# Moving the closing residual addition of a 30-step recurrence into its middle, and splitting the last stores over two queues

## The chip, the cores and the metric

The kernel runs on one core of a Trainium2 chip. The metric is the device time of one execution in microseconds (us), as the median of several runs. The engines are named as the profile names them: PE (TensorE matrix products; PEld its weight loads), DVE (VectorE), ACT (ScalarE), POOL (GpSimd) and SP (SyncE, which here only issues transfers; SPq is its queue).

## The reference

Rows of a 3327 x 256 matrix `x` go through two layers. Each layer is a graph attention over a 3327 x 3327 adjacency matrix, added to `x`, and then a network, also added to `x`. In layer 0 the network is a mixture of 16 experts; in layer 1 it is a recurrence of 30 steps. The change touches only the end of layer 1, which is, cut to what matters:

```python
def step(h, _):
    h = h + 0.01 * jnp.tanh(h)
    h = h * jax.nn.sigmoid(h)
    h = _layernorm(h, ln_w, ln_b)          # eps = 1e-5
    h = jnp.einsum('bsc,dc->bsd', h, W) + b
    return (h, None)
x = x + _L1_gnn_ref(_layernorm(x), adj, ...)
h, _ = jax.lax.scan(step, _layernorm(x), None, length=30)
x = x + h                                  # the closing addition
```

So the output is the last state of the recurrence plus the rows of `x` as they stood before the recurrence began.

## The kernel before

**Layout.** The rows lie in 26 tiles of 128 partitions x 256 features, all float32, resident in the on-chip tile `x`. For the recurrence they are handled in 7 groups: groups 0 to 5 have four tiles, group 6 has two. `COUNT` is 7, `LAST` is 30 x 7 = 210, and a number `at` from 0 to 209 stands for one group in one step. The state in `x` is kept multiplied by S = 100.

**Before the recurrence.** When the attention of layer 1 has finished some row tiles, `begin_state` stores them to the DRAM tensor `kept` (L1012, on SP) and normalizes them in place. `kept` is what the closing addition needs later. The adjacency matrix lies on chip in the tile `adjT` (13 x 3328 bfloat16 numbers on each partition) until the attention of layer 1 is through.

**One group in one step** is a `Group` object with these parts:
- `tanh` (L1050, ACT) writes `th`; `add` (L1053, POOL) adds the state to it, a 128 x 1024 addition of float32; `silu` (L1057, ACT) writes `z`.
- `measure` (L1062, L1065, DVE) takes mean and variance; `invert` (L1070 and L1071, POOL) raises variance plus eps to the power -1/2, in two small instructions, into `rr`.
- The transposed `z` is made in one of two ways. Groups 0, 2, 4 and 6 use `turn_here`: transposes on PE (L1081), copied by ACT (L1083). Groups 1, 3 and 5 use `turn_away`: ACT packs the bytes (L1090), SP stores them to DRAM (L1091) and loads them back with a transposing transfer (L1095) into `zTa`, of which there are two buffers.
- `product` (L1105, PE) multiplies by the 256 x 256 matrix `wc` into the PSUM tile `po`, of which there are two buffers. `evict` (L1115, DVE) scales each tile by `rr`, adds the bias `bb` (already times S) and writes the state back into `x`.

**Order.** The last loop of the program fixes the order of work. At each `at` it emits, in this order: `evict` of at-1, `invert` of at+3, `silu` of at+4, `turn_here` of at+2, `turn_away` and `measure` of at+4, `tanh` of at+6, `add` of at+5, `product` of at. From the second step on, `put` and `tc.keep_in_program_order` hold each engine's instructions to that order, so an instruction that waits holds back everything behind it on its engine. Transfers of `turn_away` are not held to it, but SP also issues its queue in order.

**The last step.** For `at >= LAST - COUNT`, `evict` goes on: SP loads the group's rows of `kept` into a tile `old` (L1122, two buffers), DVE computes state / S + old with one instruction over the whole group (L1123), and `move_pairs` stores the result to `out` on SP (L77). Groups 0 to 5 are one store each; group 6, which holds the ragged end of the 3327 rows, is three: 112 row pairs, 15 row pairs, and a single row.

Of the kernel before, what the change touches and what calls it, by code (L numbers as in the profile page):

```python
# [11 lines left out]
F32 = mybir.dt.float32  # L12
I32 = mybir.dt.int32
I16 = mybir.dt.int16
BF16 = mybir.dt.bfloat16
FP8 = mybir.dt.float8e4
AF = mybir.ActivationFunctionType
ALU = mybir.AluOpType
# [3 lines left out]
P = 128  # L22
ALPHA = 0.2
EPS = 1e-5
N_STEPS = 30
S = 100.0
G = 4
# [4 lines left out]
def gat_moe_gat_recurrent_ffn(ctx: ExitStack, tc: tile.TileContext, a: dict, out: bass.AP):  # L32
    nc = tc.nc
    N, D = a["x"].shape
    KD = D // P
    NT = (N + P - 1) // P
    NP = NT * P
    PAIRS = NT // 2
# [6 lines left out]
    groups = [range(t, min(t + G, NT)) for t in range(0, NT, G)]  # L45
# [25 lines left out]
    if REST < P:  # L71
        nc.vector.memset(x[:, NT - 2, :], 0.0)

    def move_pairs(dram, tile, c0, c1, into_dram):

        def move(dst, src):
            nc.sync.dma_start(*((dst, src) if into_dram else (src, dst)))  # L77

        full = min(c1, PAIRS - 1)
        if full > c0:  # L80
            move(
                dram[c0 * 2 * P : full * 2 * P, :].rearrange("(t p b) d -> p t (b d)", p=P, b=2),
                tile[:, : 2 * (full - c0), :].rearrange("p (t b) d -> p t (b d)", b=2),
            )
        if c1 == PAIRS:
            base, last = (PAIRS - 1) * 2 * P, 2 * (PAIRS - 1 - c0)
            for r0, r1 in spread(REST // 2):
                move(
                    dram[base + 2 * r0 : base + 2 * r1, :].rearrange("(p b) d -> p (b d)", b=2),
                    tile[r0:r1, last : last + 2, :].rearrange("p b d -> p (b d)"),  # L90
                )
            if REST % 2:
                move(dram[base + REST - 1 : base + REST, :], tile[REST // 2 : REST // 2 + 1, last, :])
# [212 lines left out]
    graph = ctx.enter_context(tc.tile_pool(name="graph", bufs=1))  # L306
    adj_pairs = graph.tile([P, PAIRS, NP], BF16, name="adjT")
    adjT = adj_pairs.bitcast(FP8).rearrange("p c (i b) -> p c i b", b=2)
# [714 lines left out]
    with ExitStack() as st:  # L1023
        ps_t = st.enter_context(tc.tile_pool(name="ps3t", bufs=2, space=PSUM))
        turns = cycle((ps, ps_t))
        ps_o = st.enter_context(tc.tile_pool(name="ps3o", bufs=2, space=PSUM))
        last_p = st.enter_context(tc.tile_pool(name="last", bufs=2))

        apart = [dram.tile([G * P, 2, D], I16, name=f"apart{q}") for q in range(2)]
        apart_p = st.enter_context(tc.tile_pool(name="apart", bufs=2))  # L1030

        AWAY = (1, 3, 5)
        COUNT = len(groups)
        LAST = N_STEPS * COUNT

        class Group:

            def __init__(self, at):
                self.at = at
                self.ts = groups[at % COUNT]  # L1040
                self.n = len(self.ts)
                self.hs = x[:, self.ts[0] : self.ts[0] + self.n, :]
                self.away = at % COUNT in AWAY and at > 1

            def put(self, ins):
                return tc.keep_in_program_order(ins) if self.at >= COUNT else ins

            def tanh(self):
                self.th = steps["th"].tile([P, G, D], F32, name="th")[:, : self.n, :]
                self.put(nc.scalar.activation(self.th, self.hs, AF.Tanh, scale=1.0 / S))  # L1050

            def add(self):
                self.put(nc.gpsimd.tensor_tensor(self.th, self.th, self.hs, ALU.add))  # L1053

            def silu(self):
                self.z = steps["z"].tile([P, G, D], F32, name="z")[:, : self.n, :]
                self.put(nc.scalar.activation(self.z, self.th, AF.Silu, scale=1.0 / S))  # L1057

            def measure(self):
                stats = narrow.tile([P, G, 6], F32, name="stats")  # L1060
                for j in range(self.n):
                    self.put(nc.vector.bn_stats(stats[:, j, :], self.z[:, j, :]))  # L1062
                self.v = narrow.tile([P, G, 2], F32, name="v")
                for j in range(self.n):
                    self.put(nc.vector.bn_aggr(self.v[:, j, :], stats[:, j, :]))  # L1065

            def invert(self):
                self.r = narrow.tile([P, G], F32, name="rr")
                r = self.r[:, : self.n]
                self.put(nc.gpsimd.tensor_scalar(r, self.v[:, : self.n, 1], EPS, None, op0=ALU.add))  # L1070
                self.put(nc.gpsimd.tensor_tensor(r, r, neg_half[:, : self.n], ALU.pow))  # L1071

            def turn_here(self):
                pool = next(turns)
                zT = steps["zT"].tile([P, G, KD, P], F32, name="zT")
                for c in range(self.n // 2):
                    pt = pool.tile([P, 2, KD, P], F32, name="bank")
                    for j in range(2):
                        for k in range(KD):
                            (tc.keep_in_program_order if self.at > 1 else lambda ins: ins)(  # L1080
                                nc.tensor.transpose(pt[:, j, k, :], self.z[:, 2 * c + j, k * P : (k + 1) * P], ident)  # L1081
                            )
                    self.put(nc.scalar.copy(zT[:, 2 * c : 2 * c + 2, :, :], pt))  # L1083
                self.zT = lambda j, k: zT[:, j, k, :]

            def turn_away(self):
                n = self.n
                parts = apart_p.tile([P, G, 2, D], I16, name="parts")[:, :n]
                here = apart[self.at % COUNT // 2 % 2][: n * P]
                self.put(nc.scalar.copy(parts, self.z.bitcast(I16).rearrange("p j (d b) -> p j b d", b=2)))  # L1090
                nc.sync.dma_start(  # L1091
                    here.rearrange("(j p) b d -> p j (b d)", p=P), parts.rearrange("p j b d -> p j (b d)")
                )
                zT = apart_p.tile([P, KD, G * P], F32, name="zTa")
                nc.sync.dma_start(  # L1095
                    zT.bitcast(I16)[:, :, : n * 2 * P], here.rearrange("t b d -> (t b) d"), transpose=True
                )
                self.zT = lambda j, k: zT[:, k, j * P : (j + 1) * P]

            def product(self):  # L1100
                self.po = ps_o.tile([P, G, D], F32, name="po")
                for j in range(self.n):
                    for k in range(KD):
                        tc.keep_in_program_order(
                            nc.tensor.matmul(  # L1105
                                self.po[:, j, :], lhsT=self.zT(j, k), rhs=wc[:, k, :],
                                start=(k == 0), stop=(k == KD - 1),
                            )
                        )

            def evict(self):
                ts, n = self.ts, self.n
                for j in range(n):
                    self.put(
                        nc.vector.scalar_tensor_tensor(  # L1115
                            self.hs[:, j, :], self.po[:, j, :], self.r[:, j : j + 1], bb, op0=ALU.mult, op1=ALU.add
                        )
                    )
                if self.at >= LAST - COUNT:
                    here = slice(ts[0] * P, (ts[-1] + 1) * P)  # L1120
                    old = last_p.tile([P, G, D], F32, name="old")
                    nc.sync.dma_start(old[:, :n, :], kept[here, :].rearrange("(t p) d -> p t d", p=P))  # L1122
                    nc.vector.scalar_tensor_tensor(  # L1123
                        self.hs, self.hs, 1.0 / S, old[:, :n, :], op0=ALU.mult, op1=ALU.add
                    )
                    move_pairs(out, self.hs, ts[0] // 2, (ts[-1] + 1) // 2, True)

        live = {}

        def on(at, *what):  # L1130
            if 0 <= at < LAST:
                if at not in live:
                    live[at] = Group(at)
                for w in what:
                    w(live[at])

        for at in range(-6, LAST + 2):
            on(at - 1, Group.evict)
            live.pop(at - 1, None)
            on(at + 3, Group.invert)  # L1140
            on(at + 4, Group.silu)
            on(at + 2, lambda g: g.away or g.turn_here())
            on(at + 4, lambda g: g.away and g.turn_away())
            on(at + 4, Group.measure)
            on(at + 6, Group.tanh)
            on(at + 5, Group.add)
            on(at, Group.product)


# [47 lines left out]
```

## Time and profile before

| What | Value |
|---|---|
| median of 3 runs | 1867.72 us (1865.54 to 1868.72) |
| the profiled execution: its own time / its span | 1862.0 us / 1860.3 us |
| busy shares of the span | PE 97%, PEld 89%, DVE 69%, ACT 64%, POOL 50% |
| recurrence, from its first transposes on PE | 1085 us to the end |
| stretch 1400 to 1600 us: busy us of 200 | PE 200.0, ACT 173.3, DVE 166.8, POOL 185.8 |
| last 29.8 us: busy us | PE 20.4, DVE 20.7, POOL 6.1, ACT 5.1 |
| granted PE clock, mean | 0.996 |

Times in the traces are microseconds from the start of the span, of one execution. In a timeline line the columns are: start, duration of the (possibly merged) entry, engine, line of the kernel, operation, output <- inputs, shapes, and how many instructions were merged; the bracket at the end is the time for which the engine stood idle before it and what ended that idle time.

### The profile page before, as it was taken

How to read it: one execution, taken by the hardware profiler on the slowest of the kernel's cores; microseconds unless marked ns; L12 is line 12 of the kernel's file. 1: busy time of each engine (PE TensorE's matmuls, PEld its weight loads, DVE VectorE, ACT ScalarE, POOL GpSimd, SP SyncE). 2: the span in 40 equal slices, each digit the busy share in tenths (PEclk: the TensorE clock that was granted, in tenths of full speed). 3: DMA queues.
4: the chain of work that ended last, by engine and by line, in shares of the span. 5: the costliest groups of instructions: out<-in, count | busy, mean ns of one | idle time of the engine just before them, and what ended most of it. 6: DMA issues, size and time to landing. Idle time of an engine off the chain costs nothing.

```text
span 1860.3 us, 32198 instructions
## 1 busy us (share of the span) xinstructions
PE 1809.2 (97%) x11212; PEld 1653.9 (89%) x11212; DVE 1284.7 (69%) x3829; ACT 1186.9 (64%) x1498; POOL 939.3 (50%) x864
## 2 busy tenths in 40 slices
PE   7999999999999998899999999999999999999997
PEld 6999999998999998688888888888888888888886
DVE  7888888852222222666776778888888888888887
ACT  2877777641111111556666678888888888888884
POOL 3010212255333331101111159999999999999994
PEclk9999999999999999999999999999999999999999
DMA  8898260169999885400000035554555455555557
GB/s 175 114 122 99 57 100 22 61 224 298 339 338 336 298 284 166 151 14 17 21 15 17 17 108 125 124 127 125 118 132 117 123 133 125 121 121 125 125 127 202
DMA packets 377309, 253.97 MB, mean 137 GB/s; under 512 B 238821, under 2 KB 336924, under 8 KB 377146
## 3 DMA queue, kind: packets, MB, share of 16 engines
q1 hardware_dynamic: 361026, 219.04, 43.1%
q0 software_dynamic: 11440, 28.09, 8.8%
q10 hardware_dynamic: 4680, 4.76, 0.8%
q8 instruction: 91, 1.49, 0.3%
q14 instruction: 72, 0.59, 0.1%
HBM read 168.19 MB, written 76.49 MB: 132 GB/s over the span
## 4 chain that ended last, share of the span: by engine, by line
PE 67%; issue 10%; DVE 6%; POOL 5%; DMA 5%; ACT 0%; SPq 0%; POOLq 0%; DVEq 0%; ACTq 0%
PE po L1105 35%; PE acc L286 24%; PE bank L1081 5%; DVE pT L281 3%; POOL given L855 2%; POOL rb L761 2%; DMA given<-wh,to 2%; DMA wh<-in_w_dram 1%; DMA old<-kept 1%; DMA lists<-pair,ati 1%; PE bank L835 1%; PE acc L163 1%; PE bank L526 1%; POOL rstd L121 1%; PE bank L148 0%
## 5 line engine op out<-in xcount | busy, mean ns | idle before, releaser
L276 ACT ACTIVATE e<-rb,minus,full 128x384 f32<-128x384 f32 (+3 forms) x494 | 400.1, 823 | 166.7 <-DVE pT L281 150.6
L1053 POOL TENSOR_TENSOR th<-th,x 128x1024 f32<-128x1024 f32 (+1 forms) x210 | 465.1, 2215 | 16.0 <-ACT th L1050 14.4
L281 DVE SCALAR_TENSOR_TENSOR pT<-e,part,adjT 128x384 f32<-128x384 f32 (+3 forms) x494 | 383.3, 780 | 118.8 <-PE acc L286 103.4
L1115 DVE SCALAR_TENSOR_TENSOR x<-po,rr,bb 128x256 f32<-128x256 f32 x780 | 323.0, 475 | 104.2 <-PE po L1105 67.3
L1105 PE MATMUL po<-wc,zT 128*128 128x256 f32 x1696 | 385.9, 379 | 1.2 <-DVE x L1115 1.2
L1105 PEld LDWEIGHTS po<-wc,zT 128*128 128x128 f32 x1696 | 315.1, 190 | 40.7 <-issue 1.6
L1105 PE MATMUL po<-wc,zTa 128*128 128x256 f32 x1424 | 321.9, 379 | 0.0
L286 PE MATMUL acc<-wh,pT 128*128 128x129 f32 x2704 | 309.8, 276 | 2.1 <-DVE pT L281 2.1
L286 PEld LDWEIGHTS acc<-wh,pT 128*128 128x128 f32 x2704 | 305.0, 192 | 2.7 <-DVE pT L281 2.5
L1105 PEld LDWEIGHTS po<-wc,zTa 128*128 128x128 f32 x1424 | 268.3, 190 | 35.3
L286 PE MATMUL acc<-s_wh,pT 128*128 128x257 f32 x1352 | 295.2, 381 | 3.5 <-DVE pT L281 3.3
L286 PEld LDWEIGHTS acc<-s_wh,pT 128*128 128x128 f32 x1352 | 256.0, 190 | 42.1 <-DVE pT L281 6.3
L1062 DVE BATCH_NORM_STATS2 stats<-z 128x6 f32<-128x256 f32 x780 | 275.1, 413 | 20.7 <-ACT z L1057 20.6
L1057 ACT ACTIVATE z<-th 128x1024 f32<-128x1024 f32 (+1 forms) x210 | 207.9, 990 | 76.9 <-POOL th L1053 76.7
L121 POOL TENSOR_TENSOR rstd<-ve,neg_half 128x4 f32<-128x4 f32 (+3 forms) x28 | 30.8, 1101 | 409.5 <-DVE ve L119 326.1
L1050 ACT ACTIVATE th<-x 128x1024 f32<-128x1024 f32 (+1 forms) x210 | 209.8, 1000 | 27.0 <-DVE x L1115 24.1
L1071 POOL TENSOR_TENSOR rr<-rr,neg_half 128x4 f32<-128x4 f32 (+1 forms) x210 | 208.4, 992 | 17.5
L1090 ACT COPY parts<-z 128x2048 int16<-128x2048 int16 x89 | 169.1, 1900 | 5.9 <-PE acc L286 4.0
L881 ACT ACTIVATE e<-bank 128x512 f32<-128x512 f32 x61 | 36.4, 597 | 196.3 <-PE bank L835 183.5
L885 DVE TENSOR_TENSOR pT<-e,bank 128x512 f32<-128x512 f32 x61 | 41.9, 688 | 167.5 <-PE bank L835 167.4
L835 PEld LDWEIGHTS bank<-hT,wh 128*128 128x128 f32 x1280 | 149.3, 192 | 4.9 <-ACT hT L827 1.4
L835 PE MATMUL bank<-hT,wh 128*128 128x128 f32 x1280 | 150.5, 275 | 2.4 <-DMA wh<-in_w_dram 2.4
(196 smaller groups left out, 1640.0 us busy)
## 6 DMA issues: line engine op xcount, KB each, us to landing
wh<-in_w_dram SPq DMA_DIRECT2D x120, 512.0 KB
apart<-parts SPq DMA_DIRECT2D x89, 512.0 KB
first_set<-in_w_dram SPq DMA_DIRECT2D x63, 512.0 KB
in_bytes<-in_adj_dram POOLq DMA_DIRECT2D x3, 2496.0 KB, 28.7
x<-in_x_dram SPq DMA_DIRECT2D x6, 512.0 KB
kept<-x SPq DMA_DIRECT2D x8, 384.0 KB
old<-kept SPq DMA_DIRECT2D x6, 512.0 KB
out_dram<-x SPq DMA_DIRECT2D x6, 512.0 KB
```

The lines of the kernel that those rows point to most:

```text
L276: nc.scalar.activation(e[:, : n * P], rb[:, : n * P], AF.Relu, scale=sc.full[:, j, h : h + 1], bias=sc.minus[:, j, h : h + 1],)
L281: masked = nc.vector.scalar_tensor_tensor(pT[:, : n * P], e[:, : n * P], sc.part[:, j, h : h + 1], adjT[:, j // 2, ts[0] * P : (ts[-1] + 1 ...
L286: nc.tensor.matmul(po[c], lhsT=pT[:, c * P : (c + 1) * P], rhs=wh[:, j, h, :], start=(j == 0 and c % per_bank == 0), stop=(j == NT - 1), s ...
L835: nc.tensor.matmul(p[:, f, :], lhsT=w[:, k, f * P : (f + 1) * P], rhs=hT[:, k, :], start=(k == 0), stop=(k == KD - 1),)
L1050: self.put(nc.scalar.activation(self.th, self.hs, AF.Tanh, scale=1.0 / S))
L1053: self.put(nc.gpsimd.tensor_tensor(self.th, self.th, self.hs, ALU.add))
L1057: self.put(nc.scalar.activation(self.z, self.th, AF.Silu, scale=1.0 / S))
L1062: self.put(nc.vector.bn_stats(stats[:, j, :], self.z[:, j, :]))
L1071: self.put(nc.gpsimd.tensor_tensor(r, r, neg_half[:, : self.n], ALU.pow))
L1090: self.put(nc.scalar.copy(parts, self.z.bitcast(I16).rearrange("p j (d b) -> p j b d", b=2)))
L1105: nc.tensor.matmul(self.po[:, j, :], lhsT=self.zT(j, k), rhs=wc[:, k, :], start=(k == 0), stop=(k == KD - 1),)
L1115: nc.vector.scalar_tensor_tensor(self.hs[:, j, :], self.po[:, j, :], self.r[:, j : j + 1], bb, op0=ALU.mult, op1=ALU.add)
```

## The change

Three things are altered.

1. The rows of `kept` are no longer loaded in the last step. A new function `old_rows(at)`, called once per `at` between `add` and `product`, loads one group's rows in each of the steps 6 to 12 (at the place `at % 7 == 2`, on SP), and in each of the steps 8 to 14, at the same place, adds `beside` to one group's rows on POOL. `beside` is the bias divided by S, made once by DVE. The rows lie in the room of `adjT`, which is taken again for this; the pool `last` goes. (`spaces` is defined and not used.)
2. In the last step `invert` multiplies variance plus eps by S x S, so that `rr` comes out divided by S, and `evict` adds the group's prepared rows in the place of the bias. The addition over the whole group (L1123) goes. In all other steps the first instruction of `invert` now multiplies by 1.0, where it had no second operation.
3. The stores of the last step take the queues of SP and ACT in turn, beginning with SP for each group. Only group 6 has more than one store, so its second one (15 row pairs) goes to ACT's queue.

```diff
-    def move_pairs(dram, tile, c0, c1, into_dram):
+    def move_pairs(dram, tile, c0, c1, into_dram, queues=(nc.sync,)):
+        queues = cycle(queues)
         def move(dst, src):
-            nc.sync.dma_start(*((dst, src) if into_dram else (src, dst)))
+            next(queues).dma_start(*((dst, src) if into_dram else (src, dst)))
...
-        last_p = st.enter_context(tc.tile_pool(name="last", bufs=2))
...
+        space = graph.tile([P, PAIRS, NP], BF16, name="adjT").rearrange("p c n -> p (c n)").bitcast(F32)
...
+                self.last = at >= LAST - COUNT
...
             def invert(self):
...
-                self.put(nc.gpsimd.tensor_scalar(r, self.v[:, : self.n, 1], EPS, None, op0=ALU.add))
+                self.put(nc.gpsimd.tensor_scalar(r, self.v[:, : self.n, 1], EPS, S * S if self.last else 1.0, op0=ALU.add, op1=ALU.mult))
...
             def evict(self):
-                ts, n = self.ts, self.n
-                for j in range(n):
+                ts = self.ts
+                for j in range(self.n):
+                    plus = olds[self.at % COUNT][:, j, :] if self.last else bb
                     self.put(
                         nc.vector.scalar_tensor_tensor(
-                            self.hs[:, j, :], self.po[:, j, :], self.r[:, j : j + 1], bb, op0=ALU.mult, op1=ALU.add
+                            self.hs[:, j, :], self.po[:, j, :], self.r[:, j : j + 1], plus, op0=ALU.mult, op1=ALU.add
                         )
                     )
-                if self.at >= LAST - COUNT:
-                    here = slice(ts[0] * P, (ts[-1] + 1) * P)
-                    old = last_p.tile([P, G, D], F32, name="old")
-                    nc.sync.dma_start(old[:, :n, :], kept[here, :].rearrange("(t p) d -> p t d", p=P))
-                    nc.vector.scalar_tensor_tensor(
-                        self.hs, self.hs, 1.0 / S, old[:, :n, :], op0=ALU.mult, op1=ALU.add
-                    )
-                    move_pairs(out, self.hs, ts[0] // 2, (ts[-1] + 1) // 2, True)
+                if self.last:
+                    move_pairs(out, self.hs, ts[0] // 2, (ts[-1] + 1) // 2, True, (nc.sync, nc.scalar))
+
+        beside = rec.tile([P, 1, D], F32, name="prod")
+        nc.vector.tensor_scalar(beside[:, 0, :], bb, 1.0 / S, None, op0=ALU.mult)
+        olds = [
+            space[:, (8 + i) * G * D : (9 + i) * G * D].rearrange("p (j d) -> p j d", d=D)[:, : len(ts), :]
+            for i, ts in enumerate(groups)
+        ]
+
+        def old_rows(at):
+            step, i = divmod(at, COUNT)
+            if i == 2 and 6 <= step < 6 + COUNT:
+                ts = groups[step - 6]
+                here = slice(ts[0] * P, (ts[-1] + 1) * P)
+                tc.keep_in_program_order(
+                    nc.sync.dma_start(olds[step - 6], kept[here, :].rearrange("(t p) d -> p t d", p=P))
+                )
+            if i == 2 and 8 <= step < 8 + COUNT:
+                old = olds[step - 8]
+                tc.keep_in_program_order(
+                    nc.gpsimd.tensor_tensor(old, old, beside.to_broadcast([P, old.shape[1], D]), ALU.add)
+                )
...
             on(at + 5, Group.add)
+            old_rows(at)
             on(at, Group.product)
```

More of the change, by code (lines that the diff above doesn't have):

```diff
@@ L1026, in gat_moe_gat_recurrent_ffn @@
         ps_o = st.enter_context(tc.tile_pool(name="ps3o", bufs=2, space=PSUM))
-        last_p = st.enter_context(tc.tile_pool(name="last", bufs=2))
         apart = [dram.tile([G * P, 2, D], I16, name=f"apart{q}") for q in range(2)]
         apart_p = st.enter_context(tc.tile_pool(name="apart", bufs=2))
+        space = graph.tile([P, PAIRS, NP], BF16, name="adjT").rearrange("p c n -> p (c n)").bitcast(F32)
+        spaces = [space[:, i * G * D : (i + 1) * G * D] for i in range(8)]
         AWAY = (1, 3, 5)
```

## The prediction

> **What bounds the kernel now.** I read the page first, then the timeline of the recurrence's start, one steady step, and the last 20 us.
>
> ```profile
> PE 1809.2 (97%) x11212; PEld 1653.9 (89%) x11212; DVE 1284.7 (69%) x3829; ACT 1186.9 (64%) x1498; POOL 939.3 (50%) x864
> PE   7999999999999998899999999999999999999997
> POOL 3010212255333331101111159999999999999994
> ```
>
> PE is full, so work spared on another engine is worth something only where PE waits: here, at the end. But in the recurrence POOL, 50% over the span, is at 9 tenths as well, and the change gives POOL more to do there. So I looked at how much room POOL has. Its timeline (only POOL's entries) where the recurrence settles:
>
> ```profile
> 1099.95 2.38 POOL L1053 TENSOR_TENSOR th<-th,x 128x1024 f32<-128x1024 f32 x1
> ...
> 1118.33 1.28 POOL L1053 TENSOR_TENSOR th<-th,x 128x512 f32<-128x512 f32 x1
> 1119.94 0.23 POOL L1070 TENSOR_SCALAR rr<-v 128x4 f32<-128x4 f32 x1 [0.32 <-DVE v L1065]
> ...
> 1124.60 2.36 POOL L1053 TENSOR_TENSOR th<-th,x 128x1024 f32<-128x1024 f32 x1
> 1127.21 0.23 POOL L1070 TENSOR_SCALAR rr<-v 128x4 f32<-128x4 f32 x1 [0.24 <-DVE v L1065]
> ...
> 1138.88 0.23 POOL L1070 TENSOR_SCALAR rr<-v 128x4 f32<-128x4 f32 x1 [0.63 <-DVE v L1065]
> ...
> 1150.12 2.37 POOL L1053 TENSOR_TENSOR th<-th,x 128x1024 f32<-128x1024 f32 x1
> ```
>
> The lines at 1124.60 and 1150.12 are the addition of group 1 one step apart: a step is 25.5 us. In it POOL is idle three times, 0.24 + 0.63 + 0.32 = 1.19 us. Not all of that is room. From 1099.95 to 1124.60 POOL took only 24.65 us: it was 0.87 late and caught up. In that step the 0.24 and the 0.63 were gone, but the 0.32 (at 1119.94) was still there. It follows the short 128x512 addition of group 6: the inverse of group 5 waits for silu and statistics of an addition that POOL itself made just before, so lateness moves it along unchanged. POOL can catch up **0.87 us a step**, no more.
>
> How late may POOL be before PE feels it? From a steady step (whole timeline, all engines):
>
> ```profile
> 1284.26 1.05 ACT L1057 ACTIVATE z<-th 128x1024 f32<-128x1024 f32 x1
> 1285.87 1.40 DVE L1062 BATCH_NORM_STATS2 stats<-z 128x6 f32<-128x256 f32 x4
> 1288.62 1.66 DVE L1115 SCALAR_TENSOR_TENSOR x<-po,rr,bb 128x256 f32<-128x256 f32 x4 [1.08 <-PE po L1105]
> 1290.84 3.32 PEld L1105 LDWEIGHTS po<-wc,zT 128*128 128x128 f32 x16
> ```
>
> This is the `z` of group 2, its statistics, the eviction of group 5 that stands behind them on DVE, and the product of the next group 0, which takes the `po` that this eviction frees. If `z` ends late, the statistics push the eviction. `z` ends at 1285.31; statistics and aggregates take 1.64 (as behind the `z` of group 5, where DVE waits for nothing else), four evictions 1.63, and PE starts 0.12 after the last one (as at 1850.01 to 1850.13 in the tail): 1288.70, against 1290.84. So there are **2.14 us** of slack. The same sum gives 1.8 us for group 5 (but its `z` comes after the 0.87 has been caught up), 2.6 to 3.6 for the others. ACT works without a gap from the `z` of group 1 to this one, so it arrives as late as POOL's addition of group 1.
>
> The end, from the whole timeline of the last 20 us:
>
> ```profile
> 1845.31 3.62 PE L1105 MATMUL po<-wc,zTa 128*128 128x256 f32 x16
> 1847.22 1.22 DVE L1123 SCALAR_TENSOR_TENSOR x<-x,old 128x1024 f32<-128x1024 f32 x1 [3.18 <-DMA old<-kept]
> 1848.36 1.65 DVE L1115 SCALAR_TENSOR_TENSOR x<-po,rr,bb 128x256 f32<-128x256 f32 x4
> ...
> 1850.16 1.97 PE L1105 MATMUL po<-wc,zT 128*128 128x256 f32 x8 [1.23 <-DVE x L1115]
> ...
> 1853.69 1.23 DVE L1123 SCALAR_TENSOR_TENSOR x<-x,old 128x1024 f32<-128x1024 f32 x1 [0.38 <-DMA old<-kept]
> 1854.83 0.87 DVE L1115 SCALAR_TENSOR_TENSOR x<-po,rr,bb 128x256 f32<-128x256 f32 x2
> 1854.94 3.02 SPq L77 DMA_DIRECT2D out_dram<-x  x4
> 1856.12 0.69 DVE L1123 SCALAR_TENSOR_TENSOR x<-x,old 128x512 f32<-128x512 f32 x1 [0.42 <-DMA old<-kept]
> ```
>
> DVE waits 3.18 us for an `old` load, so the eviction of group 4 is late, so PE waits 1.23 us, and two more loads and additions stand between the last product and the last stores.
>
> **The tail, part 1.** Without L1122 and L1123, group 4's eviction follows its product (which ends at 1845.48) and `po` is free by 1847.2. PE goes on from group 5 at its pace of 3.46 us per 16 matmuls: group 6 starts at 1848.77 and ends 1.89 later (its duration in a steady step), at 1850.66. Group 5's eviction ends at about 1850.7; group 6's starts 0.11 behind its product and takes 0.84: 1851.61. Now that point is 1856.12 + 0.69 = 1856.81, so 5.20 are saved. Then the stores: the third one of group 6 is issued by 1854.94 + 3.02 = 1857.96, 1.15 after 1856.81. Two on SP (0.37 and 0.24 with the gap between them) take 0.7, with the third beside them on ACT, which has nothing behind it: 0.45 saved. The remaining 2.34 to the end of the span stay. Sum: **5.65 us saved**. From below: group 5's 512 KB store ends no sooner after its issue than the 5.36 from 1854.94 to the end of the span, which makes it 1850.72 + 5.36 = 1856.1 and the gain 4.2; the trace shows 380 to 400 GB/s for such stores (1.4 us of data), so I take 5.65. From above 6.0, if ACT's store also spares SP's gaps.
>
> **POOL, part 2.** Six additions of 128x1024 and one of 128x512, one a step in steps 8 to 14, behind the addition of group 0. The nearest row is L1053, same engine, operation, shape, also in place: 2.37 us, the next instruction 2.33 after its start (1.25 for 128x512). That the second operand is one row repeated has no row. Bounds: 1.25, if only one operand costs, and 3.3, the stretch of the one 128x512 addition at 1832.71 (1.80 for 1.28) that ran beside L1123, which reads two on-chip operands; no such DVE instruction runs in steps 8 to 14, so I take 2.33. Behind each stand group 6's inverse, group 1's addition, then everything. It waits for a load issued two steps earlier, hence for nothing.
> Lateness of group 1's addition: 2.33 in the first of these steps; each step then adds 2.33 - 0.87 = 1.46. At the seventh: 6 x 2.33 + 1.25 - 6 x 0.87 = 10.0 us. PE is pushed by all of it above 2.14: **7.9 us added**, from 0.3 in the first such step, 1.5 a step after. It never gets this back, being full; afterwards only POOL recovers. DVE and ACT (83% and 86% busy) stay behind POOL.
>
> An addition of this size takes 2.37 us on POOL (L1053) and 1.23 on DVE (L1123). The Trainium skill, page GPSIMD Engine Reference, section 4.1 Engine selection, speaks against this move: it sends elementwise additions to VectorE, GpSimd being about twice as slow with two inputs. The trace agrees in the ratio. By the rule the addition would sit on DVE, idle some 4 us a step, and the sum would be the tail's gain alone, 1862.1.
>
> **The rest, part 3.** The second operation in L1070 (all 210): no POOL row has one; on DVE two operations on 128x4 take 157 ns (L119), one takes 162 (L198). I take nothing; up to 0.23 each at the far end (a second such instruction): it would fit into the 0.87 except in steps 8 to 14, where 49 of them cost up to 11 us. `beside`: one DVE instruction (L813, the same shape, 0.30), between nothing and 0.3 where DVE holds the start up; nothing taken. Loads in steps 6 to 12: SP issues 0.4 to 1.0 us each, by order after group 5's transposing load (issued 1276.19 to 1278.55); SP's next issue is at 1283.43, and the DMA share of the busy time is near zero from 1280 to 1284. Should one go ahead of that transposing load, its data come later by the load's time: data end at 1280, the product needs them at 1284.8. The loads of the tail took 3.8 to 7.2 us, there beside stores; so nothing taken, 2.4 a step in the worst case. Loads issued before step 1 (two, at 1083.3) go: nothing, SP is idle.
>
> **Sum.** -5.65 + 7.9 = +2.2 us on the span of 1860.3 (1862.0 with what lies around it), so 1864 on that execution. The median is 5.7 above it; I add the difference to the median: 1867.7 + 2.2 = 1869.9. About 0.2% (3.7 us) is what a measurement can tell from no change, so my forecast is no visible change, leaning slower.
>
> **Rivals.** *POOL's lag does not reach PE* (faster): for it, three `th` and four `z` buffers between POOL and PE, and no PE stall at the start while POOL was 0.87 late; against it, DVE's fixed order. It decides if the addition takes under 1.4 us a step or the slack is above 8 us. Time: 1867.7 - 5.65 = 1862.1.
> *POOL's step is longer than I make it* (slower): one mechanism, the repeated operand. From 2.56 us per addition on (10% longer than L1053) the whole is over 3.7 us slower; at 3.3 it adds 14.2, that is 1876.2. For it, that nothing in the trace shows this operand form; against it, that L1053 keeps to 2.36 to 2.38 with anything beside it but L1123.
>
> **Chances.** Forecast 0.46, longer POOL step 0.37 (mostly just over the line, since 1.5 us are enough), lag hidden 0.17. The forecast's own range is 1866 to 1871.4. For 8 in 10, the range goes from 1863.0 to 1876.0: it leaves out half of the faster case and the far end of the slower one.
>
> **What would show it.** In steps 8 to 14 POOL without idle time but about 0.3 a step; steps of about 27.0 us there, 25.5 before and after; PE waiting for DVE's eviction before group 0's product; the new additions at 2.37. At the end no wait of DVE for transfers, group 6's product right behind group 5's, the span ending 3.1 us after the last eviction. I am wrong if PE shows no gaps there, if L1070 or the new addition is longer, or if PE waits for `zTa`.

## The result, and the profile after

The changed kernel takes 1871.46 us (median of 22 runs), the kernel before 1867.22 us (22 runs beside them): ratio 1.0023, 95% interval 1.0017 to 1.0030. It is slower by 4.2 us. The prediction had 1869.9, 2.2 slower, and called anything up to 3.7 us no visible change; the result lies a hair beyond that line, and inside the range of 1863.0 to 1876.0.

The profiled execution of the changed kernel has a span of 1870.2 us, 9.9 more than before, but 5.9 of these lie ahead of the recurrence, whose first transposes on PE start at 1090.94 in the place of 1085.07. That start wanders between 1084.2 and 1092.5 over the executions shown below, whatever the kernel's end looks like. So profiles are compared here **from the recurrence's first transposes on PE to the end of the span**: 775.2 us before (1860.3 - 1085.07), 779.3 after (1870.2 - 1090.94). The difference, 4.0 (779.26 less 775.23), is close to the 4.2 of the timed runs.

It is made of two parts, as forecast: a middle that got longer and an end that got shorter. The middle first. The waits of the recurrence up to the last steps (all engines; columns: us in total, times, longest), before and then after:

```profile
ACT z L1057 <- POOL th L1053: 74.0, 114, 1.6
DVE stats L1062 <- ACT z L1057: 18.1, 59, 0.6
```

```profile
ACT z L1062 <- POOL th L1058: 87.0, 99, 3.7
DVE stats L1067 <- ACT z L1062: 55.8, 92, 2.5
PE po L1110 <- DVE x L1121: 6.7, 5, 1.3
```

ACT waits longer for POOL, DVE longer for ACT, and at the end of that chain PE waits for DVE, five times 1.3 us, where it had not waited once in the same stretch before. One of these five in the timeline of the changed kernel:

```profile
1340.87 1.06 ACT L1062 ACTIVATE z<-th 128x1024 f32<-128x1024 f32 x1 [3.73 <-POOL th L1058]
...
1345.06 1.04 ACT L1062 ACTIVATE z<-th 128x1024 f32<-128x1024 f32 x1
...
1346.13 1.41 DVE L1067 BATCH_NORM_STATS2 stats<-z 128x6 f32<-128x256 f32 x4 [0.94 <-ACT z L1062]
...
1347.74 1.62 DVE L1121 SCALAR_TENSOR_TENSOR x<-po,rr,bb 128x256 f32<-128x256 f32 x4
...
1349.48 3.32 PEld L1110 LDWEIGHTS po<-wc,zT 128*128 128x128 f32 x16 [1.54 <-ACT z L1062]
1349.51 3.69 PE L1110 MATMUL po<-wc,zT 128*128 128x256 f32 x16 [1.34 <-DVE x L1121]
```

This is the place that the prediction named: `z` of group 1 waits 3.73 us for POOL, `z` of group 2 follows, its statistics wait for it, the eviction of group 5 stands behind them, and group 0's product starts 0.15 after that eviction ends (1349.36). The starts of group 6's transposes in PE's timeline give the length of each step; here three of the changed kernel:

```profile
1337.15 0.60 PE L1086 MATMUL bank<-ident,z 128*128 128x128 f32 x4
1364.28 0.60 PE L1086 MATMUL bank<-ident,z 128*128 128x128 f32 x4
1391.38 0.60 PE L1086 MATMUL bank<-ident,z 128*128 128x128 f32 x4
```

A step is 25.51 us in both kernels, except for seven steps after: 25.64, 27.13, 27.10, 27.11, 27.15, 27.13, 26.02. Together they are 8.7 us too long.

The end of the changed kernel (whole timeline):

```profile
1859.87 3.62 PE L1110 MATMUL po<-wc,zTa 128*128 128x256 f32 x16
1860.14 1.66 DVE L1121 SCALAR_TENSOR_TENSOR x<-po,rr,adjT 128x256 f32<-128x256 f32 x4 [2.23 <-PE po L1110]
1863.32 1.89 PE L1110 MATMUL po<-wc,zT 128*128 128x256 f32 x8
1863.59 2.60 DVE L1121 SCALAR_TENSOR_TENSOR x<-po,rr,adjT 128x256 f32<-128x256 f32 x6 [1.79 <-PE po L1110]
1866.23 0.62 ACTq L79 DMA_DIRECT2D out_dram<-x  x1
```

PE goes from group 5 to group 6 without a gap, DVE waits for PE and never for a transfer, and the last eviction ends at 1866.19. But then 4.0 us pass to the end of the span, where before 3.5 passed (1856.81 to 1860.3). The busy time in half-microsecond stretches after that eviction (the last two columns are DMA share and GB/s):

```profile
1866.20:1866.70 0.50, 0.00 (x0) 0.00 (x0) 0.00 (x0) 0.00 (x0) 0.00 (x0) 1.00 0.99 377
1866.70:1867.20 0.50, 0.00 (x0) 0.00 (x0) 0.00 (x0) 0.00 (x0) 0.00 (x0) 1.00 1.02 385
...
1868.20:1868.70 0.50, 0.00 (x0) 0.00 (x0) 0.00 (x0) 0.00 (x0) 0.00 (x0) 1.00 0.65 236
1868.70:1869.20 0.50, 0.00 (x0) 0.00 (x0) 0.00 (x0) 0.00 (x0) 0.00 (x0) 1.00 0.00 0
```

The same view of the kernel before, from its last addition on:

```profile
1856.80:1857.30 0.50, 0.00 (x0) 0.00 (x0) 0.01 (x1) 0.00 (x0) 0.00 (x0) 0.50 0.84 311
1857.30:1857.80 0.50, 0.00 (x0) 0.00 (x0) 0.00 (x0) 0.00 (x0) 0.00 (x0) 0.50 0.24 66
...
1858.30:1858.80 0.50, 0.00 (x0) 0.00 (x0) 0.00 (x0) 0.00 (x0) 0.00 (x0) 0.50 0.53 187
1858.80:1859.30 0.50, 0.00 (x0) 0.00 (x0) 0.00 (x0) 0.00 (x0) 0.00 (x0) 0.50 0.00 0
```

After, the DMA engines are full for the first microsecond with the 512 KB of group 5, which were released only 0.9 us before; the data of group 6 come behind them. Before, they fall to a share of 0.24 in between: group 5's data were through. Read from these shares (an estimate), the last data move about 2.4 us after the last eviction, before 1.8 after the last addition; from there to the end of the span it is some 1.7 in both.

### The profile page after: what moved, and what is told of

Read it like the earlier page. It is cut to its first block, busy times and chain, and to the rows that moved or that the text cites. A ratio compares the mean times of both kernels' runs of the same rounds, so it can differ in the third digit from the quotient of the medians.

```text
span 1870.2 us, 32189 instructions
## 1 busy us (share of the span) xinstructions
PE 1815.5 (97%) x11212; PEld 1657.1 (89%) x11212; DVE 1276.6 (68%) x3823; ACT 1185.0 (63%) x1498; POOL 946.6 (51%) x871
## 4 chain that ended last, share of the span: by engine, by line
PE 62%; POOL 13%; issue 10%; DVE 6%; DMA 2%; ACT 1%; SPq 0%; another core or an unknown queue 0%; POOLq 0%; DVEq 0%; ACTq 0%
PE po L1110 28%; PE acc L288 24%; POOL th L1058 5%; PE bank L1086 4%; DVE pT L283 3%; POOL given L857 2%; PE bank L837 2%; POOL rb L763 2%; POOL rr L1076 2%; DMA given<-wh,to 2%; PE acc L165 1%; PE acc L853 1%; POOL adjT L1146 1%; PE bank L150 1%; PE bank L528 1%
## 5 line engine op out<-in xcount | busy, mean ns | idle before, releaser
L1058 POOL TENSOR_TENSOR th<-th,x 128x1024 f32<-128x1024 f32 (+1 forms) x210 | 464.6, 2212 | 16.0 <-ACT th L1055 14.4
L1121 DVE SCALAR_TENSOR_TENSOR x<-po,rr,bb 128x256 f32<-128x256 f32 x754 | 311.1, 473 | 75.5 <-PE po L1110 37.9
L1076 POOL TENSOR_TENSOR rr<-rr,neg_half 128x4 f32<-128x4 f32 (+1 forms) x210 | 204.4, 973 | 17.5
```

Source lines behind the costliest of these rows:

```text
L1121: nc.vector.scalar_tensor_tensor(self.hs[:, j, :], self.po[:, j, :], self.r[:, j : j + 1], plus, op0=ALU.mult, op1=ALU.add)
```

## The experiments

The theory was: each addition makes POOL late by its whole length, POOL catches up by a fixed amount a step, and what passes the slack of about 2.1 us pushes PE for good. Its rivals: the loads or the second operation of the inverse do it; or an addition costs PE its share wherever it stands. The table gives the ratio of times to the kernel before, the time from the first transposes to the end, and the *lag*: how much later than in `no_adds` group 6's last product starts (763.7 us behind the first transposes there).

| Run | ratio (95%) | to the end, us | lag, us |
|---|---|---|---|
| kernel before | 1 | 775.2 | (waits for DVE at the end) |
| changed kernel | 1.0023 (1.0017 to 1.0030) | 779.3 | 8.7 |
| no_adds | 0.9974 (0.9965 to 0.9983) | 770.7 | 0 |
| every_4th | 0.9976 (0.9967 to 0.9985) | 771.9 | 1.2 |
| every_2nd | 0.9997 (0.9987 to 1.0007) | 775.3 | 4.6 |
| on_dve | 0.9975 (0.9965 to 0.9984) | 770.7 | 0.0 |
| one_op | 1.0008 (1.0000 to 1.0017) | 777.7 | 7.1 |
| later_stats | 1.0014 (1.0004 to 1.0023) | 778.6 | 7.9 |
| one_queue | 1.0025 (1.0015 to 1.0034) | 779.5 | 8.8 |
| queues_only | 1.0003 (0.9993 to 1.0012) | 774.9 | as before |
| joined | 0.9978 (0.9969 to 0.9987) | 771.3 | 0.9 |
| best | 0.9963 (0.9950 to 0.9977) | 770.5 | 0.0 |

**no_adds**: the additions alone, taken away.

```diff
-            if i == 2 and 8 <= step < 8 + COUNT:
-                old = olds[step - 8]
-                tc.keep_in_program_order(nc.gpsimd.tensor_tensor(old, old, beside..., ALU.add))
```

> The seven additions on POOL are left out (the output then lacks the last bias); the loads of the kept rows in steps 6 to 12, the second operation in the inverse and the new stores stay. Measure: from the recurrence's first transposes on PE to the end of the span, 775.2 us before and 779.3 us in the changed kernel. POOL theory (additions make POOL late, DVE's order hands it to PE): no PE gap in the middle, 779.3 - 8.7 = 770.6; time 0.9975 of before. Rival, the loads in the middle hold back the transposing loads on SP, or the second operation does it: it stays at 778 to 779, ratio 1.002.

770.7 us; PE waits nowhere in the recurrence, every step is 25.51. The loads in the middle and the second operation, both still there, cost PE nothing by themselves. The whole lag comes with the additions. It also gives the worth of the tail alone: 775.23 - 770.66 = 4.6 us.

**every_4th** and **every_2nd**: the same seven additions on POOL, further apart (the loads move with them, each two steps ahead; their lines are left out).

```diff
-            if i == 2 and 8 <= step < 8 + COUNT:
-                old = olds[step - 8]
+            k = (step - 3) // 4                    # every_2nd: (step - 8) // 2
+            if i == 2 and (step - 3) % 4 == 0 and 0 <= k < COUNT:
+                old = olds[k]
```

> The same seven additions on POOL, in steps 3, 7, ..., 27 in place of 8 to 14 (each load two steps ahead of its addition). POOL theory: each addition makes POOL 2.35 us late, it catches up about 0.75 a step, so 3.0 before the next; lateness never adds up and passes the slack of 2.14 by 0.2 at most: 770.8 us from the first transposes to the end, ratio 0.9975. Rival, each addition costs PE its share wherever it stands (contention, or POOL's total work): as in the changed kernel, 779, ratio 1.002.

> The seven additions on POOL in steps 8, 10, ..., 20. A dose between the changed kernel (every step) and every fourth step. POOL theory, with 0.75 us caught up a step: lateness 6 x 2.35 + 1.25 - 12 x 0.75 = 6.35, less 2.14 = 4.2; with 770.7 without lateness that is 774.9 us from the recurrence's first transposes to the end of the span, time about as before (ratio 1.000). Rival, what counts is only whether there is an addition in a step (seven pushes of one size): as in the changed kernel, 779, or as every fourth step, 771 to 772.

The lag is 1.2 and 4.6 us against 0.2 and 4.2 expected, and 8.7 with an addition in each step. The work on POOL is the same in all three, so it isn't the work that costs but its spacing: lateness adds up when the next addition comes before the last has been caught up. In every_4th the steps of the first five additions are 25.64 to 25.65 us: each addition lets 0.14 us through, which puts the slack at 2.35 - 0.14 = 2.2 us. (The expectation counted its 0.2 only once, though PE never gets a push back; in joined, below, the step of each of the six long additions is 25.65 to 25.66.) The step of the sixth addition is 26.10. There PE also waited in front of group 1's product:

```profile
1710.15 3.69 PE L1110 MATMUL po<-wc,zTa 128*128 128x256 f32 x16 [0.23 <-DMA zTa<-apart]
```

`z` of group 1 was late by the addition, and so were its store and its transposing load: a second way from POOL to PE, which later_stats meets again. Why it was too late only here, in one of six like steps, is not explained. In every_2nd five steps are 26.40 to 26.43, which is 0.9 too long, each the remainder of two steps; group 0's product again starts 0.15 behind group 5's eviction (1373.18 after 1373.03), though the view names ACT's `z` there.

**on_dve**: the additions on the other engine, at the same places.

```diff
-                    nc.gpsimd.tensor_tensor(old, old, beside.to_broadcast([P, old.shape[1], D]), ALU.add)
+                    nc.vector.tensor_tensor(old, old, beside.to_broadcast([P, old.shape[1], D]), ALU.add)
```

> The seven additions on DVE, at the same places in steps 8 to 14. POOL theory: DVE has some 4 us idle in a step and 3.06 us of slack at this place, the addition takes about 1.23 there; POOL may stand still for part of it (0.5 to 1.2 us a step, against 0.75 that it catches up), so 770.6 to 771.7 us from the first transposes to the end, ratio 0.9975 to 0.998. Rival, DVE's evictions come late instead and PE waits as before: 1.2 a step, 779, ratio 1.002.

No step is longer than 25.51 and the time is that of no_adds: on DVE the additions cost PE nothing, and the tail's gain alone is left. They do make POOL late, as the last section shows, but not by more than the slack.

**one_op**: the second operation only where it is needed.

```diff
-                self.put(nc.gpsimd.tensor_scalar(r, ..., EPS, S * S if self.last else 1.0, op0=ALU.add, op1=ALU.mult))
+                if self.last:
+                    self.put(nc.gpsimd.tensor_scalar(r, ..., EPS, S * S, op0=ALU.add, op1=ALU.mult))
+                else:
+                    self.put(nc.gpsimd.tensor_scalar(r, ..., EPS, None, op0=ALU.add))
```

> The second operation of the inverse's first instruction only in the last step, none before. POOL theory: the additions are the cause, the second operation only takes 0.12 us a step from what POOL can catch up; lateness 15.35 - 6 x 0.87 = 10.1, less 2.14 = 8.0 instead of 8.7, so 778.6 us from the first transposes to the end, ratio 1.002. Rival, the second operation is the larger part: 773 or less, ratio 0.999 or less.

The lag falls from 8.7 to 7.1, by twice as much as expected; the additions stay the larger cause by far. What the second operation costs can't be read from its duration. POOL's timeline of the changed kernel, and then of one_op:

```profile
1261.90 2.37 POOL L1058 TENSOR_TENSOR th<-th,x 128x1024 f32<-128x1024 f32 x1
1264.35 0.19 POOL L1075 TENSOR_SCALAR rr<-v 128x4 f32<-128x4 f32 x1
1264.63 1.02 POOL L1076 TENSOR_TENSOR rr<-rr,neg_half 128x4 f32<-128x4 f32 x1
1265.62 2.37 POOL L1058 TENSOR_TENSOR th<-th,x 128x1024 f32<-128x1024 f32 x1
```

```profile
1315.90 2.38 POOL L1058 TENSOR_TENSOR th<-th,x 128x1024 f32<-128x1024 f32 x1
1318.25 0.22 POOL L1078 TENSOR_SCALAR rr<-v 128x4 f32<-128x4 f32 x1
1319.56 2.37 POOL L1058 TENSOR_TENSOR th<-th,x 128x1024 f32<-128x1024 f32 x1
```

(In the second, L1079 stands between the last two lines and is left out.) With two operations the instruction reads 0.19 in the place of 0.22, but it starts 2.45 behind the addition in the place of 2.35, and from one addition to the next it is 3.72 against 3.66. The durations say faster, the starts say slower, and the starts are right: in one_op a step in which POOL is full takes 26.86 us, in the changed kernel 27.12. (Five inverses that are 0.05 to 0.06 longer and group 6's, 0.09 longer, make more than 0.26; POOL's wait behind the short addition is 0.34 in one_op and 0.28 in the changed kernel, which takes a part back.)

**later_stats**: DVE's order altered, to test the last link.

```diff
-            on(at + 3, Group.invert)
+            on(at + 2, Group.invert)
...
-            on(at + 4, Group.measure)
+            on(at + 3, Group.measure)
```

> The changed kernel with DVE's order altered: the statistics of a group are taken one place later (behind the next eviction), and its inverse on POOL one place later too. The additions stay in steps 8 to 14. If lateness reaches PE through the statistics that stand ahead of group 5's eviction on DVE, that slack of 2.14 us falls away and the next one is that of the transposes of z (about 4.5); POOL's fixed wait of 0.27 behind the short addition goes as well, so it catches up about 1.0 a step: lateness 15.35 - 6 x 1.0 = 9.3, less 4.5 = 4.8 instead of 8.7; 775 to 776 us from the first transposes to the end, against 779.3; ratio to before 1.000. Rival, POOL's lateness reaches PE some other way (the inverse, the tanh): 778 or more, ratio 1.002.

The expectation failed in its size. The wait of PE for DVE before group 0's product is gone, as it had to be if that link carried the lag, but another came in its place (waits of PE):

```profile
PE po L1110 <- DMA zTa<-apart: 6.5, 5, 2.4
```

PE now waits before the products of the away groups, for rows that were stored and transposed by transfers: late `z` means late stores. I had put the next slack at 4.5 and it is hardly wider than the first one. POOL's wait behind the short addition is gone too, yet its step stays at 27.0 us. Of the 0.27 only 0.17 could go: from the start of the short addition to the inverse it is 1.37 in the place of 1.54, the rest being the usual distance between two instructions. The next addition starts 0.07 later behind its inverse, so 0.1 is left. So: that lateness passed over DVE's order in the changed kernel is shown by where PE waits; that loosening this order would help much is refuted.

**one_queue** and **queues_only**: the two store queues, undone and done alone.

```diff
-                    move_pairs(out, self.hs, ..., True, (nc.sync, nc.scalar))     # one_queue, on the changed kernel
+                    move_pairs(out, self.hs, ..., True)
```

> The changed kernel with all stores on SP. The prediction's own step says that ACT's queue saves 0.45 us: last eviction to the end of the span would go from 4.0 to 4.45 us. Rival, the end is set by the data of group 5's store, which go first and with which those of group 6 queue up: 4.0 to 4.1, no difference. A third, ACT's store is itself the late one: 3.5 to 3.8.

> The kernel before with only part 3 of the change, the second store of group 6 on ACT. There the data of group 5's store are through before those of group 6 start, so that the issue can count: by the prediction's step 3.49 us from the last addition to the end become 3.0 to 3.1, and 775.2 from the first transposes to the end 774.8. Rival, the store on ACT takes as long as two in a row on SP: 3.4 to 3.6. No change of time that timed runs can tell, ratio 1.000.

In one_queue the last eviction ends at 1861.50 and the span at 1865.6: 4.1 us, against 4.0 with both queues. In queues_only (whole timeline):

```profile
1858.74 0.69 DVE L1125 SCALAR_TENSOR_TENSOR x<-x,old 128x512 f32<-128x512 f32 x1 [0.38 <-DMA old<-kept]
1859.47 0.62 ACTq L79 DMA_DIRECT2D out_dram<-x  x1
```

From 1859.43 to the end at 1863.0 it is 3.6, against 3.5 without. An issue on ACT takes 0.62 us, two in a row on SP take 0.75 in the changed kernel; so the second queue does not bring the end nearer here, whether data of group 5 are still in front or not. What it does shorten is the issuing: in one_queue the last issue is through 1.5 us after the last eviction (1860.59 + 2.42), in the changed kernel 0.8 (1866.22 + 0.75). In one_queue the rival with group 5's data holds and the one with a late store on ACT (3.5 to 3.8) falls; in queues_only the rival holds.

**joined** and **best**: versions meant to beat both kernels.

```diff
                     )
-                if self.last:
-                    move_pairs(out, self.hs, ts[0] // 2, (ts[-1] + 1) // 2, True, (nc.sync, nc.scalar))
+                    if self.last and j % 2:
+                        c = (ts[0] + j) // 2
+                        move_pairs(out, self.hs[:, j - 1 : j + 1, :], c, c + 1, True, (nc.sync, nc.scalar))
```

with one_op's edit in both, every_4th's additions in joined and on_dve's in best.

> A version meant to beat both: the additions on POOL in steps 3, 7, ..., 27, the second operation of the inverse only in the last step, and in the last step a store behind every second eviction (one pair of tiles each, SP first, then ACT only for the ragged end), so that the data of group 5's first half start 0.85 us sooner. POOL theory: no lateness reaches PE. If the data of group 5's store set the end, last eviction to end falls from 4.1 to about 3.3: 769.9 to 770.2 us from the first transposes to the end, ratio 0.997 of before. If issue or completion sets it, 4.0 to 4.4 stays: 770.7 to 771, ratio 0.9975.

> The additions on DVE in steps 8 to 14, the second operation of the inverse only in the last step, and in the last step a store behind every second eviction. POOL theory: no step is longer than 25.5 us, so group 6's last product starts 763.7 us after the first transposes (1 us sooner than with the additions on POOL in every fourth step, each of which let 0.14 through); with 2.6 for the two groups' evictions and 3.8 to the end, 770.3 to 770.5, ratio 0.997.

joined missed: 771.3 where at most 770.2 was expected with the split store. The 0.14 us of each addition add up to 0.9, and from the last eviction to the end it is 3.8 where 3.3 was hoped for. Timed, it can't be told from no_adds. best is as expected: 770.5, group 6's product after 763.7, 3.9 us from the last eviction to the end. It has the lowest ratio, 0.9963, but its interval overlaps those of joined, on_dve and every_4th, and from the first transposes to the end it is only 0.2 us ahead of on_dve.

## Why the prediction was right, and where it was not

**The tail up to the last eviction** (5.20 forecast): 771.7 us behind the first transposes before (1856.81 - 1085.07), 766.6 in no_adds (1859.10 - 1092.54), a difference of 5.2. Each of its sub-steps shows in the lines of the changed kernel above.

**The stores** (0.45 forecast): this step failed. From the last eviction to the end 3.5 us became 4.0 to 4.1: 0.6 lost where 0.45 were to be gained. The issuing went about as forecast; it is through 0.8 us after the last eviction (1866.97), 1.15 before. Wrong was that "the remaining 2.34 to the end of the span stay": 3.2 pass now, because the data of group 6 end later, 2.4 us after the last eviction in the place of 1.8. The prediction had the reason at hand, group 5's 512 KB going first, as its lower bound of 4.2 for the whole tail, and put it aside because those data last only 1.4 us. The tail is worth 4.6, not 5.65. That group 5's data are all of it is not shown: joined and best, which release half of them sooner, still need 3.8 and 3.9.
The Trainium skill, page DMA: Bandwidth & Descriptors, section Issuing engines are not separate DMA queues, says that a second issuing engine saves only the time of the issue. one_queue agrees: with both queues the issuing is through 0.7 us sooner behind the last eviction, and the end, 4.0 against 4.1, comes hardly sooner.

**The addition on POOL** (2.33 from start to next start): right. The repeated operand costs nothing extra, 2.38 like L1058's 2.37, and the rival that rested on it falls:

```profile
1305.62 2.37 POOL L1058 TENSOR_TENSOR th<-th,x 128x1024 f32<-128x1024 f32 x1
1307.94 2.38 POOL L1146 TENSOR_TENSOR adjT<-adjT,prod 128x1024 f32<-128x1024 f32 x1
1310.40 0.19 POOL L1075 TENSOR_SCALAR rr<-v 128x2 f32<-128x2 f32 x1
...
1331.47 0.19 POOL L1075 TENSOR_SCALAR rr<-v 128x4 f32<-128x4 f32 x1 [0.28 <-DVE v L1070]
...
1335.06 2.38 POOL L1146 TENSOR_TENSOR adjT<-adjT,prod 128x1024 f32<-128x1024 f32 x1
```

The one idle time of POOL that was said to stay, behind group 6's short addition, is there with 0.28, and it is the only one between the two additions.

**What POOL catches up** (0.87 a step): mis-sized. The kernel that the prediction worked with is one_op's, as it took the second operation at nothing; there the full step is 26.86, and the instruction behind the new addition starts 2.35 after it (1308.91 to 1311.26), so POOL catches up 25.51 - (26.86 - 2.35) = 1.00. The 0.87 came from the one step at the start of the recurrence in which POOL happened to be just that late: it was the lateness that was there to catch up, not the most that could be. The kernel before shows it:

```profile
1110.93 2.38 POOL L1053 TENSOR_TENSOR th<-th,x 128x1024 f32<-128x1024 f32 x1
1113.36 0.23 POOL L1070 TENSOR_SCALAR rr<-v 128x4 f32<-128x4 f32 x1
```

The inverse starts 2.43 behind the addition, where 2.33 is POOL's own pace: 0.10 of the wait that the prediction took to be gone was still there. With 1.00 the forecast's sum gives 7.1 in the place of 7.9, and one_op measures 7.1.

**The second operation in the inverse** (nothing): wrong. 8.7 - 7.1 = 1.6 us, the 0.26 by which a full step is longer, six times. DVE's rows, from which it was taken at nothing, say nothing about POOL. With it POOL catches up only 25.51 - (27.12 - 2.35) = 0.74 a step.

**The slack of 2.14 us** and its place: right; every_4th puts it at 2.2. **The loads, `beside`, the kept order**: nothing, as no_adds shows.

So -4.6 + 8.7 = +4.1 stands where -5.65 + 7.9 = +2.2 had been forecast. The mechanism holds: POOL's lateness adds up over consecutive steps and reaches PE over DVE's order, at the place and past the slack that were named. Three sizes were off: the store step and the second operation were priced too kindly, by 1.05 and 1.6 us, and the catch-up too low by 0.13 a step, 0.8 the other way. That the last took back part of the first two is luck. One sign of being wrong did come, L1070 longer, though in its spacing and not in its duration; and past its line of 3.7 us the prediction had put the rival *POOL's step is longer than I make it*. POOL's step is longer, but by the second operation and not by the repeated operand that the rival rested on. The rival *lag does not reach PE* has its time, 0.9974, only in the versions that take the additions off POOL or spread them.

## What to carry to other kernels

An engine that is busy 93% of a periodic loop, as POOL is here, has room for what it can catch up in one period, and that is less than its idle time: 1.0 us a step in one_op, 0.74 in the changed kernel, where 1.19 were idle before. Work beyond that, given in consecutive periods, adds up, and once it passes the slack of the chain behind, the full engine pays and never gets it back. The same work cost 8.7 us in consecutive steps, 4.6 in every second, 1.2 in every fourth, and nothing on DVE. Before moving work into a "hidden" place, count the idle time there that lateness can eat, and spread the work by it.

## What was not expected of the hardware

DVE and POOL seem to wait for each other when DVE reads two on-chip operands. From on_dve (whole timeline):

```profile
1303.52 2.36 POOL L1058 TENSOR_TENSOR th<-th,x 128x1024 f32<-128x1024 f32 x1
...
1304.78 2.19 DVE L1146 TENSOR_TENSOR adjT<-adjT,prod 128x1024 f32<-128x1024 f32 x1
...
1305.97 1.05 POOL L1075 TENSOR_SCALAR rr<-v 128x2 f32<-128x2 f32 x1
```

DVE's addition reads 2.19 us, but 1.09 of them come after POOL's addition has ended at 1305.88; the same amount of work (L1123) took 1.23 in the kernel before. Then POOL's small instruction, 0.19 elsewhere, takes 1.05, to 1307.02, just past the end of DVE's at 1306.97. The other five long additions read alike (2.18 to 2.20, and 1.05). In the kernel before it is POOL that stands behind:

```profile
1832.15 1.22 DVE L1123 SCALAR_TENSOR_TENSOR x<-x,old 128x1024 f32<-128x1024 f32 x1
1832.71 1.80 POOL L1053 TENSOR_TENSOR th<-th,x 128x512 f32<-128x512 f32 x1
```

POOL's addition, 1.28 elsewhere, ends 1.14 after DVE's instruction has ended at 1833.37. The Trainium skill, page GPSIMD Engine Reference, section 8 Key points, names this: the two engines share their interfaces to on-chip memory, with contention when DVE has two such inputs. The runs agree, and show that it looks like waiting in turn rather than both being slowed.

So each long addition on DVE makes POOL 0.86 late, more than the 0.74 that it catches up in a step. Group 1's additions on POOL come 25.7 us apart in these steps, and after the sixth POOL is 1.7 late: just inside the slack of 2.2, so that PE feels nothing. At this pace (0.17 a step more, an estimate) three more such additions in a row would have reached it.
